# Gathering 17 instead of 13 target tiles in a graph network's first attention, most of them while the edge table is made

## The chip, the cores and the metric

The kernel runs on one core of a Trainium2 chip. The metric is the device time of one execution in microseconds. A core has TensorE (PE) for matrix products, VectorE (DVE), ScalarE (ACT) and GpSimd (POOL) for the rest, and SyncE (SP), which here only issues DMAs. Each engine takes its own instructions in the order in which they stand; semaphores tie the engines together. On-chip memory is SBUF, with 128 partitions, and PSUM, into which PE writes.

## The reference

There are 3125 nodes with 256 features and 50000 edges, sorted by target. Four graph layers alternate with four feed-forward blocks. Only the first graph layer and the routing behind it matter here:

```python
src, dst = with_self_loops(edge_index)
h = (x @ W.T).reshape(N, 4, 64)                # x is layer-normalized
e = leaky_relu(a_s[src] + a_d[dst], 0.2)       # a_s, a_d: one score a node and head
p = exp(e - segment_max(e, dst)[dst])
alpha = p / segment_sum(p, dst)[dst]
out = segment_sum(alpha[:, :, None] * h[src], dst)
x = x + elu(out + bias) + x_normalized
# then: layer norm, a router over 8 experts, the top 2 with their weights, their outputs added
```

## The kernel before

The 3125 nodes are 25 tiles of 128 rows, held in SBUF as `x`. The first graph layer, `gnn0`, has these stages.

*Projection.* Each tile is normalized, turned, and multiplied by the weights; `prepare` turns the scores into exponentials and writes the rows, with their scores, to DRAM as `scored` (ACT's queue).

*Edge table.* `table` makes a matrix with one column per target and one row per source that counts edges, in DRAM, for the first 19 of the 25 target tiles (`CONV`), which later convolutions use too. It goes over 152 windows of 16 targets. VectorE compares key numbers and writes one-hot tiles in 16 bits: `hi` for two windows at a time (L560, 128 x 2400), `lo` for eight windows (L552, 128 x 3072). PE multiplies them (L566, three products a window, into `pa`), ACT copies the counts to `cols` (L571), and SP writes blocks of 24 windows to DRAM (`ct<-cols`). Ten further comparisons, `same` (L478), count degrees. The table's function opens its own pools and closes them at its end.

*First attention*, `attend4`. A target tile is treated in one of two ways.

- Dense: `sweep` takes four target tiles at a time (a chunk). For each of the 25 source tiles it makes four `v` on VectorE (L857, maximum of two exponentials times the column of the table `c`, 128 x 512) and multiplies them on PE with the source rows (L917) and the denominators' row (L924). The table's columns come from DRAM by SP (`c<-ct`, five loads a chunk).
- Gathered: `GatheredAttention` fetches the rows of the actual edges. A target tile has 20 gathers of 128 rows, indirect DMAs on GpSimd's queue (L1873, `edge<-scored,from`), four to a buffer, with six buffers (`AHEAD`). Its five steps `some` each wait for the four gathers of a buffer: VectorE makes `factor` (L1921) and, in three steps of five, the product `edge<-edge,factor` (L1929); in the other two ACT makes it (L1926, 16 instructions); PE sums up (L1936, four products a step). `begin` makes the 0/1 matrices `hot` and `columns` first, for which SP loads `columns<-turned`.

Tiles from number `FIRST` on are gathered, 12 of 25 are dense, in three chunks. When a gathered step is due is set by due times: `times` has a start number, the time per tile (`each`), a delay and the time of the whole (`whole`), in planned microseconds; `upto(share)` runs all steps that are due at that share. The share is that of the dense steps done:

```python
steps += n
apart.upto(steps / (apart.start * NT))
for _ in range(apart.pace):
    if rest and s > 0:
        rest.pop(0)()
```

When two tiles are done, `experts.front` gives the pieces that route them (norm, transposes, router, place, and the sends to the experts' slots, two indirect DMAs a tile on GpSimd's queue, L2265); they go into `rest` and are run one or two after each dense step. After the last one come `schedule` and the first expert block.

A scheduler of the language then puts the instructions of each engine in an order of its own, by dependencies; the numbers of edges per target are prepared in `edges_by_column` for `GROUPED` groups of 32 targets, from tile `APART` on.

The call in `gnn0` stands after the table:

```python
early.close()
self.table(keep)
...
psum = self.pool(inner, "g0aps", 3, space=PSUM)
self.attend4(
    inner, "g0a", psum, hv, target, True, self.real, 1, done, self.scored[0],
    (FIRST, 30.0, -24.0, 420.0, 2), experts.front,
)
```

Of the kernel before, what the change touches and what calls it, by code (L numbers as in the profile page):

```python
# [32 lines left out]
P = 128  # L33
# [16 lines left out]
APART = 12  # L50

FIRST, SECOND, THIRD, CONV = 12, 12, 17, 19
# [31 lines left out]
class Net:  # L84
# [376 lines left out]
    def count_degrees(self, ctx, c):  # L461
# [28 lines left out]
        def sums():  # L490
# [7 lines left out]
            pm = one.tile([P, 512], F32, name="pm")  # L498
# [31 lines left out]
    def table(self, keep):  # L530

        nc = self.nc
        with ExitStack() as ctx:
            others = self.count_degrees(ctx, keep)
            acc = self.pool(ctx, "tabacc", 4, space=PSUM)
            lows = self.pool(ctx, "tablow", 2)
            hot = self.pool(ctx, "tabhot", 3)
            out = self.pool(ctx, "tabout", 2)  # L540
            keys = NT * WIN
            few, two = 8, 2
            block, end = 3 * P // WIN, CONV * P // WIN
            for w0 in range(0, end, block):
                n = min(block, end - w0)
                cols = out.tile([P, NT, block * WIN], BF16, name="cols")
                for w in range(w0, w0 + n):
                    if w % few == 0:
                        four = [P, few // two, P, two * TILES]
                        lo = lows.tile(four, BF16, name="lo")  # L550
                        of = self.lowt[:, w : w + few, :]
                        nc.vector.tensor_tensor(  # L552
                            lo, of.rearrange("p (q two) j -> p q (two j)", two=two).unsqueeze(2)
                            .to_broadcast(four),
                            self.keys6.unsqueeze(1).to_broadcast(four), op=ALU.is_equal,
                        )
                    if w % two == 0:
                        four = [P, two, keys, TILES]
                        hi = hot.tile(four, BF16, name="hi")
                        nc.vector.tensor_tensor(  # L560
                            hi, self.keyt[:, w : w + two, :].unsqueeze(2).to_broadcast(four),
                            self.keys3.unsqueeze(1).to_broadcast(four), op=ALU.is_equal,
                        )
                    pa = acc.tile([P, 512], F32, name="pa")
                    for j in range(TILES):
                        nc.tensor.matmul(  # L566
                            pa[:, :keys], lo[:, w % few // two, :, w % two * TILES + j],
                            hi[:, w % two, :, j],
                            start=(j == 0), stop=(j == TILES - 1),
                        )  # L570
                    nc.scalar.copy(  # L571
                        cols[:, :, (w - w0) * WIN : (w - w0 + 1) * WIN],
                        pa[:, :keys].rearrange("p (t d) -> p t d", d=WIN),
                    )
                    if others and w % 12 == 11:
                        others.pop(0)()
                nc.sync.dma_start(
                    self.ctm[:, :, w0 * WIN : (w0 + n) * WIN], cols[:, :, : n * WIN]
                )

# [247 lines left out]
    def sweep(self, ctx, name, nh, psum, hv, target, begin, step, finish, apart):  # L828
# [11 lines left out]
        def target_rows(t0, n):  # L840
            return self.target_rows(qpool, psum, target, t0, n, wide)
# [3 lines left out]
        q, rest = target_rows(*chunks[0]), []  # L845
        apart.rest = rest
        for i, (t0, n) in enumerate(chunks):
# [3 lines left out]
            for s in range(NT):  # L851
# [12 lines left out]
                apart.upto(steps / (apart.start * NT))  # L864
# [25 lines left out]
    def attend4(self, ctx, name, psum, hv, target, loops, need, flag, done, rows, times,  # L890
                ready=None):
# [6 lines left out]
        accp = self.pool(ctx, name + "acc", 1, space=PSUM)  # L898
# [57 lines left out]
        apart = GatheredAttention(self, ctx, name, psum, rows, target, times, finish_apart)  # L956

# [73 lines left out]
    def gnn0(self, experts):  # L1031
        nc, x = self.nc, self.x
        with ExitStack() as ctx:
# [5 lines left out]
            with ExitStack() as inner:  # L1039
                early = inner.enter_context(ExitStack())  # L1040
                keep = self.pool(inner, "tab", 1)
# [6 lines left out]
                edges = self.edges_by_window(inner, work, keep)  # L1048
# [23 lines left out]
                self.table(keep)  # L1072
            experts.begin(ctx)
            for load in experts.open_weights(0):
                load()

            def done(t, num, inv):
                rows = wk.tile([P, NH, HC], F32, name="rows")
                for h in range(NH):
                    nc.scalar.mul(rows[:, h, :], num[:, h, :], inv[:, h : h + 1])  # L1080
                r = rows.rearrange("p h c -> p (h c)")
                nc.vector.tensor_add(r, r, bias)
                grown = wk.tile([P, D], F32, name="grown")
                nc.scalar.activation(grown, r, AF.Exp)
                nc.scalar.activation(r, r, AF.Relu)
                nc.vector.tensor_add(x[:, t, :], x[:, t, :], r)
                nc.vector.scalar_tensor_tensor(
                    x[:, t, :], grown, 1.0, x[:, t, :], op0=ALU.min, op1=ALU.add
                )
# [1583 lines left out]
```

## Time and profile before

| | us |
|---|---|
| median of 3 runs | 4599.88 (4595.12 to 4603.21) |
| time of the profiled execution | 4597.16 |
| its span | 4595.4 |
| `hi` compares, first and last start | 106.0, 267.9 |
| first free gather, last gather (start) | 270.8, 694.6 |
| `v`, first and last start | 286.0, 738.6 |

Over the whole span PE is busy for 3727.8 us, DVE for 2503.1, POOL for 1625.9, ACT for 1221.7. Busy time of POOL counts its indirect DMAs[...], not the data's movement, and not the gap before the next issue. The median time of a gather is 1.010 us in the first attention, the shortest 0.942, the longest 6.762. The DMA column is the mean share in which the core's 16 DMA engines are busy.

### The profile page before, as it was taken

To read this page: it belongs to the slowest core of one execution; us is meant where nothing else is said; L and a number is where in the kernel's file an instruction comes from. 1 tells how busy PE (TensorE), PEld (TensorE's weight loads), DVE (VectorE), ACT (ScalarE), POOL (GpSimd) and SP (SyncE) were. 2 spreads that over 40 slices of the span, in tenths; PEclk is the share of its full clock that TensorE was granted. 3 is DMA by queue.
4 is the path that set the end of the run, shared out by engine and by line. 5 is a ranking of instruction groups with operands and counts; after the bars stand their busy time and mean duration, and the time that the engine had idled before them with its cause. 6 is when DMAs were issued, how large, how long until landed. Compare 5 with 4: busy or idle time off the path is not lost. (4 is left out here: it accounts for less than half of the span.)

```text
span 4595.4 us, 73195 instructions
## 1 busy us (share of the span) xinstructions
PE 3727.8 (81%) x25845; PEld 2022.9 (44%) x25942; DVE 2503.1 (54%) x8078; ACT 1221.7 (27%) x3841; POOL 1625.9 (35%) x1566
## 2 busy tenths in 40 slices
PE   5867775968887899999998999976599996865994
PEld 3322222543222667445444555544355554543552
DVE  7977886457765566767667421144432224533333
ACT  2433442323433111434333211100033332100331
POOL 2057772215774670000000365455311111463111
PEclk8889887989998999999998999998799998986997
DMA  4244433233443650000000465564511115443113
GB/s 125 86 143 120 122 104 92 79 109 108 126 123 94 168 144 19 2 2 2 2 2 27 140 169 165 150 216 121 147 32 29 29 29 164 130 137 81 54 52 108
DMA packets 356530, 431.28 MB, mean 94 GB/s; under 512 B 73207, under 2 KB 294063, under 8 KB 356161
## 3 DMA queue, kind: packets, MB, share of 16 engines
q0 software_dynamic: 73600, 199.97, 15.6%
q1 hardware_dynamic: 259344, 203.33, 15.2%
q10 hardware_dynamic: 23216, 23.17, 1.6%
q8 instruction: 217, 3.56, 0.3%
q14 instruction: 153, 1.25, 0.1%
HBM read 337.35 MB, written 90.59 MB: 93 GB/s over the span
## 5 line engine op out<-in xcount | busy, mean ns | idle before, releaser
L1873 POOL DMA_INDIRECT edge<-scored,from x680 | 770.3, 1133 | 482.5 <-PE pa L566 190.7
L1980 POOL DMA_INDIRECT edge<-rows,from x480 | 460.6, 960 | 338.7 <-issue 116.8
L2483 POOL DMA_INDIRECT results<-y,to x168 | 163.4, 973 | 892.9 <-DVE y L2482 580.7
L2477 PE MATMUL py<-w,ht 128*128 x1568 | 428.5, 388 | 21.1 <-DVE y L2482 17.6
L1668 PE MATMUL pz<-lstm_v,hist 128*32 128x192 f32 x7120 | 382.8, 333 | 30.5 <-DVE hist L1766 10.4
L2450 PE MATMUL ph<-w,xt 128*128 x896 | 385.9, 563 | 23.2 <-issue 12.6
L2469 ACT ACTIVATE ht<-pt,par 128x128 f32<-128x128 f32 x784 | 267.2, 366 | 442.1 <-PE pt L2466 441.7
L1926 ACT ACTIVATE edge<-edge,factor 128x65 f32<-128x65 f32 (+1 forms) x896 | 234.1, 348 | 432.6 <-DVE factor L1921 415.5
L1385 PE MATMUL acc<-c,hs 128*128 128x512 bf16 (+1 forms) x1458 | 328.7, 370 | 2.7 <-issue 1.3
L1430 PE MATMUL acc<-hs,c 128*128 128x512 bf16 x896 | 318.6, 398 | 5.2 <-DMA c<-ct 4.0
L2477 PEld LDWEIGHTS py<-w,ht 128*128 128x128 f32 x1568 | 259.2, 190 | 72.2 <-DVE y L2482 32.5
L1701 PE MATMUL pz<-pre,ident 128*128 128x192 f32 x900 | 268.6, 382 | 11.8 <-PEq L1774 11.8
L1793 POOL MEMSET hall<- 128x128 f32 x1 | 0.2, 204 | 772.3 <-DMA L_ffn_br<-in_L_ffn_br 772.3
L1434 PE MATMUL acc<-hs,c 128*128 128x256 bf16 x950 | 268.6, 283 | 4.6 <-issue 1.7
L2455 DVE COPY h<-ph 128x512 f32<-128x512 f32 (+1 forms) x224 | 139.7, 624 | 233.2 <-PE ph L2450 227.8
L1668 PEld LDWEIGHTS pz<-lstm_v,hist 128*32 128x32 f32 x7120 | 186.1, 109 | 181.3 <-DVE hist L1766 149.6
L2265 POOL DMA_INDIRECT slots<-rows,sloti x150 | 159.3, 1062 | 213.2 <-DVE sloti L2221 133.6
L2450 PEld LDWEIGHTS ph<-w,xt 128*128 128x128 f32 x896 | 158.1, 192 | 173.3 <-issue 113.0
L917 PE MATMUL acc<-v,g0hv 128*64 128x512 f32 x600 | 184.7, 712 | 58.6 <-DVE v L857 57.8
L1936 PE MATMUL edgeacc<-edge,hot 128*32 128x264 f32 (+1 forms) x1360 | 132.1, 427 | 112.5 <-DVE edge L1929 89.3
L857 DVE SCALAR_TENSOR_TENSOR v<-q,g0hv,c 128x512 f32<-128x512 f32 x300 | 216.7, 741 | 1.7 <-DMA c<-ct 1.6
L1385 PEld LDWEIGHTS <-hs 128*128 128x128 bf16 x1500 | 146.6, 99 | 158.6 <-issue 7.9
(489 smaller groups left out, 6349.2 us busy)
## 6 DMA issues: line engine op xcount, KB each, us to landing
c<-ct SPq DMA_DIRECT2D x116, 640.0 KB
slots<-slots SPq DMA_DIRECT2D x168, 129.0 KB
got<-results SPq DMA_DIRECT2D x24, 768.0 KB
w<-in_L_ffn_W SPq DMA_DIRECT2D x16, 1024.0 KB
ct<-cols SPq DMA_DIRECT2D x6, 2400.0 KB
c<-ct SPq DMA_DIRECT2D x25, 480.0 KB
edge<-scored,from POOLq DMA_INDIRECT x680
rows<-new ACTq DMA_DIRECT2D x20, 512.0 KB
```

Of the source, the lines that this page charges most:

```text
L857: nc.vector.scalar_tensor_tensor(to, q[:, h, :w], hv[:, s, h, D // nh + 1 : D // nh + 2], cols[s], op0=ALU.max, op1=ALU.mult,)
L1385: made = self.nc.tensor.matmul(acc[f][:, : n * P], lhs, cols[s], start=(s == 0 and i == 0), stop=(s == NT - 1), skip_group_check=True,)
L1430: nc.tensor.matmul(acc[t], lhs, hs[:, s, 0:2, :].rearrange("p i d -> p (i d)"), start=start, stop=stop, skip_group_check=True,)
L1434: return nc.tensor.matmul(acc[t][:, D:], lhs, hs[:, s, 2, :], start=False, stop=stop, skip_group_check=True,)
L1668: made = nc.tensor.matmul(pz[q * R : (q + 1) * R, :], s, m, start=start, stop=stop, tile_position=(0, q * R),)
L1701: made = nc.tensor.matmul(pz, self.ident, pre[:, g, s, :], start=True, stop=False)
L1873: nc.gpsimd.indirect_dma_start(out=tile[:, g, :], out_offset=None, in_=self.rows, in_offset=bass.IndirectOffsetOnAxis(ap=index, axis=0),)
L1926: nc.scalar.mul(part, part, factor[:, g, h : h + 1])
L1980: self.net.nc.gpsimd.indirect_dma_start(out=tile, out_offset=None, in_=self.rows, in_offset=bass.IndirectOffsetOnAxis(ap=index, axis=0),)
L2450: nc.tensor.matmul(ph[:, :wide], st["xt"][:, k, :], st["w1"][:, k * hid + c0 : k * hid + c0 + wide], start=(k == 0), stop=(k == KD - 1),)
L2469: nc.scalar.activation(ht[:, m, :], pt[:, cut], AF.Gelu, bias=st["par"][:, m : m + 1])
L2477: nc.tensor.matmul(py[:, :D], st["ht"][:, m, :], st["w2"][:, m * D : (m + 1) * D], start=(m == 0), stop=(m == nhc - 1),)
```

## The change

`APART` and `FIRST` go from 12 to 8: eight tiles are dense, in two chunks, and 17 are gathered. `table` no longer runs as a whole: it returns a list of 152 functions, one a window. They run in `attend4`, after the gathered attention has issued its first gathers, and after each of them the gathered steps that are due by then are run, and one waiting piece of the routing. The windows count for 0.57 of the planned time, the dense steps for the rest. The planned times change from (30, -24, 420) to (30, 6, 530). The table's pools move to the other side of SBUF, its blocks have 16 windows instead of 24, `pa` two PSUM buffers instead of four, `hi` two instead of three, and `pm` comes from the attention's pool. The experts' first weights get their memory earlier; their loads are called after the table.

```diff
-APART = 12
-FIRST, SECOND, THIRD, CONV = 12, 12, 17, 19
+APART = 8
+FIRST, SECOND, THIRD, CONV = 8, 12, 17, 19
...
-            pm = one.tile([P, 512], F32, name="pm")
+            pm = psum.tile([P, 512], F32, name="tp")
...
-            acc = self.pool(ctx, "tabacc", 4, space=PSUM)
+        acc = self.pool(ctx, "tabacc", 2, space=PSUM)
-            hot = self.pool(ctx, "tabhot", 3)
+        hot = self.pool(ctx, "tabhot", 2)
...
-            block, end = 3 * P // WIN, CONV * P // WIN
-            for w0 in range(0, end, block):
+        block, end = 2 * P // WIN, CONV * P // WIN
+        now = {}
+        def window(w):
+            if w % block == 0:
+                now["cols"] = out.tile([P, NT, block * WIN], BF16, name="cols")
...
+            if others and w % 12 == 11:
+                others.pop(0)()
+            if i == block - 1 or w == end - 1:
                 nc.sync.dma_start(
-                    self.ctm[:, :, w0 * WIN : (w0 + n) * WIN], cols[:, :, : n * WIN]
-                )
+                    self.ctm[:, :, (w - i) * WIN : (w + 1) * WIN], cols[:, :, : (i + 1) * WIN]
+                )
+        return [lambda w=w: window(w) for w in range(end)]
...
-        q, rest = target_rows(*chunks[0]), []
-        apart.rest = rest
+        q, rest = target_rows(*chunks[0]), apart.rest
...
-                apart.upto(steps / (apart.start * NT))
+                apart.upto(apart.share + (1 - apart.share) * steps / (apart.start * NT))
...
         apart = GatheredAttention(self, ctx, name, psum, rows, target, times, finish_apart)
+        if ahead:
+            ahead(apart)
+        accp = self.pool(ctx, name + "acc", 1, space=PSUM)
...
+            def ahead(apart):
+                with ExitStack() as ctx, self.tc.using_default_side("right"):
+                    windows = self.table(ctx, keep, psum)
+                    for i, window in enumerate(windows):
+                        window()
+                        apart.share = 0.57 * (i + 1) / len(windows)
+                        apart.upto(apart.share)
+                        if apart.rest:
+                            apart.rest.pop(0)()
+                edges.close()
+                for load in loads:
+                    load()
...
-                    (FIRST, 30.0, -24.0, 420.0, 2), experts.front,
+                (FIRST, 30.0, 6.0, 530.0, 2), experts.front, ahead,
```

## The prediction, made before the changed kernel had run

> **What bounds the kernel now.** The change touches the span up to the first expert block, about 806 us of 4595, so I read that stretch alone: first the busy time of each engine in its stages, then what VectorE and GpSimd wait for, then single instructions. The stages: the edge table is made (106 to 270 us), a turn-around (270 to 286), the dense steps of the first attention with the gathered targets among them (286 to 742), a tail (742 to 806).
>
> ```profile
> core 0: us, PE busy (x) PEld busy (x) DVE busy (x) ACT busy (x) POOL busy (x), PEclk, DMA share, GB/s
> 106.00:270.00 164.00, 137.41 (x533) 56.01 (x533) 163.54 (x110) 73.32 (x149) 6.23 (x1) 0.88 0.29 91
> 270.00:286.00 16.00, 4.73 (x29) 2.07 (x27) 6.26 (x17) 5.40 (x15) 9.02 (x9) 0.65 0.88 251
> 286.00:742.00 456.00, 343.45 (x1993) 93.91 (x1993) 357.55 (x991) 174.75 (x664) 342.97 (x294) 0.87 0.40 112
> 742.00:806.00 64.00, 18.97 (x70) 13.72 (x71) 30.34 (x145) 14.28 (x45) 11.42 (x14) 0.58 0.37 117
> ```
>
> The table is VectorE's alone (163.5 of 164 us), and GpSimd stands still in it. In the dense stage no engine looks full. But gaps between GpSimd's DMA issues are not counted as busy:
>
> ```profile
> 279.00:695.00 416.00, 329.65 (x284) 0.87 0.44 122
> ```
>
> ```profile
> DVE factor L1921 <- DMA edge<-scored,from: 78.7, 32, 5.8
> ```
>
> ```profile
> POOL edge L1873 <- issue: 63.7, 209, 0.3
> ```
>
> The first line is POOL alone in that stretch (busy, issues, clock, DMA), the others are waits from 286 to 742 (total, times, longest): 284 issues in 416 us, 329.65 us busy, and a gap of 0.30 us before each (63.7/209) makes 86 us more: 416. GpSimd is full from 279 to 695 us, at 1.465 us an issue, and VectorE loses 78.7 us waiting for gathered rows. So before, VectorE bounds the table, GpSimd the dense stage. Overlapping the two is what the change tries.
>
> What an issue costs beside a busy VectorE decides. The timeline of GpSimd and that of VectorE (start, us, engine, line):
>
> ```profile
> 263.77 6.76 POOL L1873 DMA_INDIRECT edge<-scored,from  x1 [190.67 <-PE pa L566]
> 270.84 0.95 POOL L1873 DMA_INDIRECT edge<-scored,from  x1 [0.30 <-issue]
> 283.21 1.97 POOL L1873 DMA_INDIRECT edge<-scored,from  x1 [0.30 <-issue]
> ```
>
> ```profile
> 262.72 6.98 DVE L560 TENSOR_TENSOR hi<-keyt,keys3s 128x2400 bf16<-128x2400 f16 x4
> 269.74 0.31 DVE L2159 COPY rows<-rowsto 128x2 f32<-128x2 f32 x3
> 283.12 1.24 DVE L1929 TENSOR_TENSOR edge<-edge,factor 128x1040 f32<-128x1040 f32 x1
> ```
>
> An undisturbed gather takes 0.95 us. The one at 283.21 began 0.09 us into a product of two SBUF tiles and took 1.97: it stood until the product's end (284.36) and then ran about 0.82. The one at 263.77, the only gather beside the table's compares, took 6.76: it stood through four `hi` compares and ended 0.8 us after the last. So a gather begun inside a two-input VectorE instruction waits for its end, and a run of 16-bit compares back to back was passed by in one piece. Over the dense stage the hold is 329.65/284 - 0.95 = 0.21 us an issue.
>
> **The change, part by part.** The sum is made against the profiled execution (span 4595.4, its time 4597.2, 2.7 below the median of the three runs, 4599.9).
>
> *Removed.* One of three dense chunks: 100 `v` at 0.683 us of spacing (four take 2.74), 68 us of VectorE, a third of L917 and L924 (94 us of PE), 5 loads `c<-ct`, 4 `q` copies.
>
> *Added.* Four gathered targets: 80 gathers on GpSimd, 20 `some` steps; a target costs VectorE some 6.5 us (three products at 1.17, five `factor` at 0.13, `hot` 0.75, `columns` 0.32, sum 0.34, the rest small), 26 us. Scaling on ACT is 32 x 0.336 = 10.7 us a target, PE 20 x 0.44 = 9, both on engines under half busy there. Four `columns` loads on SP of 160 KB. The per-target end (bias, exponent, normalization, routing, two sends) is done for every target either way.
>
> *Moved.* In the order in which the changed program's instructions stand, 48 of the 85 `some` steps, 204 GpSimd issues (192 gathers, 12 sends), and most of the matching front pieces come before the last `hi`. VectorE's list from first to last `hi` adds up to 279 us at the durations before (165 before); between last `hi` and first `v` 12; in the dense steps 221 (372 before). Total 512 against 544: 32 us less.
>
> *Start.* The scored rows are issued to DRAM until 100.2 us before. After, three `hi` and two `lo` stand ahead of the last of them, and the five `same` that stood there go later: I take 108 us for the first free gather; by then VectorE has done some 17 of its 279 us. Left: 262 us for 48 steps, 5.45 a step.
>
> *Table stage.* Each step needs 204/48 = 4.25 issues at 0.95 + 0.30 = 1.25 us when nothing holds them. Of the 5.45 us, 3.4 are 16-bit compares (76 `hi` at 1.745, 19 `lo` at 1.66, 10 `same` at 1.15, less those before the start), and in the order they stand in 91 runs, 1.9 a step. If a run is passed by whole, GpSimd gets in at each run's end, and about 0.35 times more in the other work: 2.25 issues. The other two run while VectorE waits for its rows: 2 x 1.25 = 2.5 us. A step takes 5.45 + 2.5 = 7.95 us, the stage 48 x 7.95 = 382, to 490 us. This is the wait that the change adds: `factor` on gathered rows, now with the next compares behind it on VectorE, the table's products on PE and its copies on ACT behind those. The whole table goes at the gathers' pace, 2.5 us a window instead of 1.08.
>
> Here a rule of the Trainium skill speaks otherwise. "SBUF — State Buffer", section "Who interferes with whom", has `tensor_tensor` without a two-port mode, contending with GpSimd's reads alone, and infers that descriptor generation needs the write interface. By that inference gathers run free beside `hi`: 204 x 1.25 = 255, so VectorE sets the stage at about 285 us (92% used). The rows say that an indirect DMA is held; it has an index to read, which would fit the page's first half. I take the rows.
>
> *Turn-around and dense stage.* From last `hi` to first `v` 16 us before (the wait for the last table write, 2.4 MB blocks and a 0.8 MB one; now ten blocks, the last again 0.8 MB): taken as equal. The remaining 168 issues (148 gathers, 20 sends) at 1.44 (a little under 1.465, since fewer products stand beside them) are 242 us, and after the last gather stand the last step and 12 `v`, 18 us: 260 from the end of the table. VectorE has 12 + 221 = 233 of work in it, so GpSimd still sets it. End at 490 + 260 = 750, against 742: +8.
>
> *Tail.* 64 us before; one more front pair stands in it (VectorE's list 26.3 against 20.9 us, with its chain through PE): +6.
>
> *Costed at nothing.* Two PSUM buffers for `pa` instead of four and two for `hi` instead of three: PE needs 0.9 us and ACT 0.49 a window, VectorE makes one in 1.08 now and 2.5 then; without that cover 0.2 us a window, 30 us. SP: `columns` loads stand among the table's writes, so a write waits behind a `columns` buffer that frees only with a gathered target; `cols` has two buffers of 16 windows (40 us at the new pace), and a block lost there costs up to one step, 8 us, once. The grouped numbers on 68 rows instead of 52 take the same instructions; `turned` is 2.8 MB instead of 2.1, 5 us more at the 122 GB/s of that stretch, needed some 30 us later. Expert weights, later attentions and convolutions keep their sizes.
>
> Sum: +8 + 6 = +14: 4611 for the profile, 4614 for the median.
>
> **The rivals.**
> 1. *The hold lets go at every compare's end* (place: each `hi`-`hi` boundary in the table stage). Then about 2.75 issues fit into the 5.45 us and 1.5 x 1.25 = 1.9 follow: 7.35 a step, 353 us, to 461; dense end 721, -21 + 6 = -15: 4585. For it: in the dense stage nearly all held gathers start at the next boundary, `v` to `v` too. Against: three boundaries passed at 263.77. It decides from 2.5 issues per step within VectorE's work: there the step is 7.7 us, the stage 368, and the sum with the tail zero.
> 2. *No hold, the page's inference*: 285 to 393, dense 260, end 653, -89 + 6: 4517. Against: both held rows.
> 3. *Compares and the small instructions between them hold as one run*: one issue a step gets in, 3.25 x 1.25 = 4.1 follow, 9.5 a step, 458 us; end 826, +90: 4690. For it: `factor` and the products have two SBUF inputs too, and stand back to back with `hi`. Against: gathers get in between products and `v` in the dense stage.
> 4. *It does not overlap*: the steps stand in the program before the last `hi`, but if rows land late enough that every step stops ACT, PE and the compares behind it, it joins case 3.
>
> **How the numbers follow.** Chances: forecast 0.34 (its own range 4595 to 4640), rival 1 0.28 (4560 to 4605), rival 2 0.13 (4500 to 4550), rival 3 with 4 0.25 (4650 to 4720). A measurement can tell about 0.2%, 9 us. Faster by more: all of rival 2, two thirds of rival 1, a little of the forecast's low end: 0.35. Within: 0.11. Slower: 0.54. The range, 4520 to 4695, leaves out half of rival 2 and the upper part of rival 3. It is wide because one row alone shows a gather beside compares.
>
> **What would show it.** Mean of the gathers before the last `hi`: near 1.6 us for the forecast (382/204 less the gap of 0.30), 1.4 rival 1, 1.1 or less rival 2, 1.9 rival 3. Last `hi` near 490; VectorE's wait for gathered rows some 120 us in the table stage; last `v` near 745; tail 70. The prediction is wrong if the last `hi` ends before 440 (the hold was overrated) or after 540, if in the dense stage GpSimd has gaps, or if the difference lies behind the first expert block.

## The result, and the profile after

The changed kernel takes 4616.52 us (median of 13 runs, 4607.79 to 4629.92) against 4601.45 for the kernel before, measured beside it (13 runs, 4595.12 to 4608.77): a ratio of 1.0035, with a 95% interval from 1.0025 to 1.0045. It is slower by 0.35%, about 16 us. The profiled execution took 4629.92 us, the longest of its 13, so I compare the two traces by the times at which things happen and not by their spans. At the first product of the first expert block (`ph`) the changed kernel is 14.4 us behind (807.6 against 793.2 us); what its profile loses after that (18.4 us more by the end of the span) is not in the medians.

The busy time of each engine by stage, of the kernel after (per window: length, then busy us and instructions of PE, weight loads, DVE, ACT, POOL, then the granted clock, the DMA share and the rate). The stages are: up to the first gather; the table with the gathered steps between its windows; the turn-around to the first `v`; the dense steps; the tail.

```profile
88.00:130.00 42.00, 4.09 (x86) 2.61 (x87) 20.97 (x26) 0.76 (x3) 0.30 (x1) 0.50 0.44 131
130.00:477.00 347.00, 219.44 (x1480) 88.01 (x1480) 253.10 (x433) 171.28 (x560) 283.63 (x209) 0.66 0.46 132
477.00:509.00 32.00, 9.04 (x46) 4.66 (x44) 13.03 (x43) 11.95 (x41) 24.08 (x27) 0.50 0.73 218
509.00:742.00 233.00, 200.10 (x1224) 55.71 (x1224) 212.27 (x549) 92.44 (x350) 177.95 (x146) 0.94 0.42 110
742.00:808.00 66.00, 14.54 (x59) 11.93 (x60) 35.24 (x175) 10.93 (x38) 14.03 (x15) 0.51 0.20 67
```

Read the POOL column of the second line: 209 issues, 283.63 us busy, 1.357 us each. With the gap of 0.30 us before each one (next fence) this is 209 x 1.66 = 347 us, the whole stage: GpSimd is full, while VectorE works for 253 of 347 us. In the dense stage and the turn-around 163 issues run from 476 to 723 us, 1.514 us each; VectorE works for 212 of the 233 us of the dense stage, so both are close to full there. The last dense product ends at 740.9, where it ended at 741.7 before. So 4 targets more and most of the gathers moved, and the dense stage ends at the same time. The loss arises after it: the tail is 66.7 us to the first `ph`, against 51.5.

The waits from 120 to 477 us (engine, line, what it waited for: total us, times, longest):

```profile
DVE factor L1946 <- DMA edge<-scored,from: 64.8, 21, 7.7
...
POOL edge L1898 <- DMA scored<-g0hv: 55.8, 1, 55.8
ACT cols L572 <- DMA turned<-short: 54.0, 1, 54.0
POOL edge L1898 <- issue: 51.5, 169, 0.3
...
DVE hi L560 <- PE pa L566: 40.9, 4, 39.5
```

The first row is the wait that the change adds, VectorE's for gathered rows: 64.8 us. The second, third and fifth are one thing that the forecast did not have: the first gather waits for the scored rows until 129.70 us, ACT's first copy of the table waits for the write of the grouped numbers (`turned<-short`), and through PE and its two buffers `pa` VectorE's `hi` waits too, 39.5 us at a stretch. GpSimd's timeline (start, us, engine, line, idle before it and what ended that):

```profile
129.70 0.98 POOL L1898 DMA_INDIRECT edge<-scored,from  x1 [55.81 <-DMA scored<-g0hv]
130.98 0.96 POOL L1898 DMA_INDIRECT edge<-scored,from  x1 [0.30 <-issue]
...
166.37 1.40 POOL L1898 DMA_INDIRECT edge<-scored,from  x1 [0.30 <-DMA edge<-scored,from]
```

And VectorE's timeline at the last of these:

```profile
165.16 3.54 DVE L560 TENSOR_TENSOR hi<-keyt,keys3s 128x2400 bf16<-128x2400 f16 x2
168.63 0.18 DVE L1946 TENSOR_TENSOR factor<-factor,edge 128x16 f32<-128x16 f32 x1
```

Two `hi` stand back to back from 165.16 to 168.70; the first ends at 166.99. The gather begun at 166.37 ended at 167.77, 0.79 us after the first `hi` and well inside the second. It got in at the boundary between two compares. So it goes for most gathers of this stage. Of the 101 gathers that have a `hi` or `lo` beside them 0.25 us after their start, 84 ended 0.79 to 0.83 us after the end of that one compare, 15 ended before it did and were not held, and two ended 2.53 us after it. Most of those compares have no other compare directly behind, so they say little about runs. Of the seven held gathers that have one, five got in at the boundary, and the two of 2.53 us stood through the next compare as well. The row on which the forecast rested, a gather that stood through four compares, is the other case. It is no accident of one trace: the first gather stands through four `hi` in all three profiles in which the table runs as a whole (6.76 us before, 6.79 in e2_rows68 and in e8_more). Why that one does not get in is not known.

### The profile page after: what moved, and what is told of

Same layout as the page of the kernel before. It is cut to its first block, busy times and chain, and to the rows that moved or that the text cites. A ratio compares the mean times of both kernels' runs of the same rounds, so it can differ in the third digit from the quotient of the medians.

```text
span 4628.2 us, 72963 instructions
## 1 busy us (share of the span) xinstructions
PE 3683.4 (80%) x25694; PEld 2015.9 (44%) x25694; DVE 2460.0 (53%) x8031; ACT 1243.0 (27%) x3962; POOL 1761.2 (38%) x1646
## 5 line engine op out<-in xcount | busy, mean ns | idle before, releaser
L1898 POOL DMA_INDIRECT edge<-scored,from x760 | 907.0, 1193 | 370.0 <-issue 203.3
L1951 ACT ACTIVATE edge<-edge,factor 128x65 f32<-128x65 f32 (+1 forms) x1024 | 267.5, 348 | 389.7 <-DVE factor L1946 356.0
L1453 PE MATMUL acc<-hs,c 128*128 128x512 bf16 x950 | 338.0, 400 | 4.8 <-DMA c<-ct 3.6
L1961 PE MATMUL edgeacc<-edge,hot 128*32 128x264 f32 (+1 forms) x1520 | 157.9, 456 | 134.8 <-DVE edge L1954 97.1
L566 PE MATMUL pa<-hi,lo 128*128 128x400 bf16 x456 | 156.5, 492 | 101.3 <-DVE hi L560 48.2
L1012 PE MATMUL acc<-g1bhv,v 128*128 128x257 f32 x850 | 204.5, 395 | 14.6 <-DVE v L860 8.4
```

The source lines that it names most:

```text
L1012: nc.tensor.matmul(a[:, : D + 1], v[0][:, j * P : (j + 1) * P], hv[:, s, 0, : D + 1], start=(s == 0), stop=(s == NT - 1),)
L1453: nc.tensor.matmul(acc[t], lhs, hs[:, s, 0:2, :].rearrange("p i d -> p (i d)"), start=start, stop=stop, skip_group_check=True,)
L1898: nc.gpsimd.indirect_dma_start(out=tile[:, g, :], out_offset=None, in_=self.rows, in_offset=bass.IndirectOffsetOnAxis(ap=index, axis=0),)
L1951: nc.scalar.mul(part, part, factor[:, g, h : h + 1])
```

## The experiments

The experiments fall into three groups of four, each with the kernel before measured beside it: 4596.75 us for e1 to e4, 4963.91 for e5 to e8, 4605.38 for e9 to e12. The second group ran on another chip, 8% slower for every kernel measured there; only its ratios are set beside the others.

| run | edit | us | ratio to before, 95% interval |
|---|---|---|---|
| after | the change | 4616.52 | 1.0035 [1.0025, 1.0045] |
| e1_split | `turned` written in two DMAs | 4608.98 | 1.0030 [1.0018, 1.0042] |
| e2_rows68 | before, 68 grouped rows | 4594.30 | 0.9996 [0.9988, 1.0004] |
| e3_short | `short` in memory of its own | 4615.85 | 1.0045 [1.0032, 1.0059] |
| e4_ten | 15 gathered targets | 4590.70 | 0.9990 [0.9981, 0.9998] |
| e5_ten48 | e4, fewer steps in the table | 4947.06 | 0.9966 [0.9951, 0.9982] |
| e6_twelve | 13 gathered targets, overlap alone | 4937.67 | 0.9940 [0.9917, 0.9963] |
| e7_halves | after, compares split in two | 4978.11 | 1.0024 [1.0008, 1.0040] |
| e8_more | before, 17 gathered targets | 5051.42 | 1.0175 [1.0153, 1.0198] |
| e9_halves | as e7_halves | 4602.22 | 1.0000 [0.9985, 1.0015] |
| e10_ten_halves | e4 and split compares | 4576.24 | 0.9937 [0.9917, 0.9957] |
| e11_twelve_halves | e12 and split compares | 4577.39 | 0.9943 [0.9921, 0.9965] |
| e12_twelve | as e6_twelve | 4592.74 | 0.9981 [0.9968, 0.9994] |

### The late start: e1_split, e2_rows68, e3_short

After, the first gather starts at 129.7 us where 108 was forecast. The suspect is the write of the grouped numbers, one DMA over 68 rows.

e1_split writes them in two pieces:

```diff
-        nc.sync.dma_start(
-            self.turned.rearrange("(w r) e -> w r e", r=GROUP),
-            short.unsqueeze(1).to_broadcast([GROUPED, GROUP, MANY * P]),
-        )
+        views = self.turned.rearrange("(w r) e -> w r e", r=GROUP)
+        for w0, w1 in ((0, 64), (64, GROUPED)):
+            nc.sync.dma_start(
+                views[w0:w1],
+                short[w0:w1].unsqueeze(1).to_broadcast([w1 - w0, GROUP, MANY * P]),
+            )
```

> The changed kernel with one edit: the write of `turned` (68 rows) is issued as two DMAs of 64 and 4 rows. Theory A (the 68-row write runs on few DMA engines, and scored rows, `columns` loads and the memory of `short` wait for it): the write lands near 105 us instead of 145, the first gather starts near 108 instead of 130, ACT's first `cols` copy no longer waits 54 us, last `hi` near 455 instead of 475, and the time is 20 to 30 us under the changed kernel, near 4590. Theory B (the scored rows are late because compares stand ahead of them): the first gather stays near 130, the time stays near 4616.

e2_rows68 gives the kernel before the 68 rows and nothing else of the change:

```diff
-APART = 12
+APART = 8
```

> The kernel before with APART = 8 alone: 68 grouped rows are prepared and written, FIRST stays 12, so nothing else moves. Theory A: the write takes some 60 us here too (landing near 145 instead of under 110); if `cols` lies in the memory of `short`, the table starts up to 36 us late (4637), otherwise nothing waits for it before 270 us and the time stays at 4601. Theory B: no difference in the write, 4601.

e3_short takes from ACT the reason to wait, by giving `short` memory that `cols` does not use again:

```diff
-        short = c.tile(sides, BF16, name="short")
+        short = keep.tile(sides, BF16, name="short")
```

> The changed kernel with `short` in the pool that lives on, so that `cols` cannot lie in its memory; the slow write stays. Theory A: ACT's 54 us wait and VectorE's 40 us stall in `hi` vanish, but the first gather stays at 130 and GpSimd sets the pace after it; VectorE has some 40 us more of compares done before the first gather, which takes hold time off the gathers (up to 18 us). Time between 4595 and 4612. If VectorE's stall itself set the time, 40 us less, near 4576.

Busy time by windows of e2_rows68, with the DMA share as the last column but one:

```profile
85.00:100.00 15.00, 6.83 (x245) 6.47 (x247) 14.39 (x19) 0.77 (x3) 0.00 (x0) 0.50 0.42 125
...
115.00:130.00 15.00, 13.37 (x48) 5.26 (x47) 15.00 (x10) 7.63 (x16) 0.00 (x0) 1.00 0.25 72
```

The same of the kernel before, with 52 rows:

```profile
85.00:100.00 15.00, 7.27 (x300) 7.08 (x300) 14.46 (x18) 0.77 (x3) 0.00 (x0) 0.50 0.77 203
...
115.00:130.00 15.00, 12.47 (x43) 4.89 (x42) 15.00 (x9) 6.89 (x14) 0.00 (x0) 0.89 0.00 0
```

And of e1_split:

```profile
85.00:100.00 15.00, 3.58 (x13) 1.78 (x13) 14.61 (x18) 0.77 (x3) 0.00 (x0) 0.50 0.84 170
```

In e2_rows68 the share from 115 to 130 us is 0.25: 4 of 16 engines, with the rest of this write and what was left of the scored rows. Before, the share was 0.77 from 85 to 100 and 0.00 from 115 on. In e1_split it is 0.84 at once, and ACT no longer waits for `turned`. The updates of the write's semaphore in the traces count the engines: behind the one at its issue come 4 in e2_rows68, the last at 141.2 us, and 13 before, the last at 100.5. The Trainium skill ("DMA: Bandwidth & Descriptors", section "Why a DMA increments its semaphore by 16 and not by 1") has a rule that fits: a DMA is spread over the largest number up to 16 that divides the size of the slowest dimension on both of its sides. For 68 rows that is 4, for 64 it is 16, for 52 it is 13; the share of 0.25 and the counts of 4 and 13 agree.

e2_rows68 also shows what this does to the scored rows. With nothing changed but the rows, the last update for them comes at 128.5 us, where it came at 111.1 before. It is 128.9 in after, and 110.5 in e12_twelve, with the overlap but 52 rows. So it is the write of 68 rows, and not the compares that now stand ahead, that makes the scored rows late. The total is no slower in e2_rows68 (0.9996), since there no gather starts before 264 us: the slow write costs only what the overlap makes wait for it.

What the start is worth e1_split does not show cleanly. It was expected near 4590, with the first gather near 108 us, and both failed. Its first gather goes at 122.7 us, released by another wait: the scheduler put VectorE's ten `same` ahead of `parts` there. Without that it could have gone little sooner, as the last of the scored rows is written at 121.9; why they are no sooner there, with the write quick, is open.

```profile
122.72 1.27 POOL L1900 DMA_INDIRECT edge<-scored,from  x1 [49.18 <-DVE parts L1862]
```

Of the 7 us gained the longer holds behind it took back 5 (206 issues of 1.684 us in the table stage instead of 209 of 1.658), the first `ph` came 1.9 us earlier than after, and the intervals of the two ratios overlap. The other kernels agree that the rows are the cause of most of the delay: the first gather starts at 129.7, 130.3, 125.9 and 126.0 us in the four profiles with the overlap and 68 rows in one write (after, e3_short, e7_halves, e9_halves), at 113.4 and 111.6 with 60 rows (15 engines; e4_ten, e10_ten_halves) and at 111.3 and 111.2 with 52 rows (e12_twelve, e11_twelve_halves).

In e3_short ACT's wait for `turned` is gone, and `hi` no longer waits for `pa`, but VectorE waits as long for the other user of the same write, the first `columns`:

```profile
DVE columns L1921 <- DMA columns<-turned: 40.4, 1, 40.4
```

The first gather, the pitch (the time from one issue to the next, 1.662 us) and the last dense product (741.2 us) stay, and the time of 4615.85 us lies above the expected 4595 to 4612. One reader of a late write was freed, and the next in the same queue took its place.

### The number of targets: e4_ten, e8_more, e6_twelve and e12_twelve, e5_ten48

e4_ten gathers 15 targets:

```diff
-APART = 8
+APART = 10
-FIRST, SECOND, THIRD, CONV = 8, 12, 17, 19
+FIRST, SECOND, THIRD, CONV = 10, 12, 17, 19
-                (FIRST, 30.0, 6.0, 530.0, 2), experts.front, ahead,
+                (FIRST, 30.0, 6.0, 470.0, 2), experts.front, ahead,
```

> The changed kernel with APART = FIRST = 10 and 470 planned microseconds: 15 gathered targets, 60 grouped rows, 10 dense targets in three chunks. Theory A: 60 rows spread over many DMA engines, so the write is quick and the first gather starts near 108; 40 gathers fewer on GpSimd (at 1.44 to 1.70 us each 60 us), VectorE 20 us more: end of the dense steps near 690, 4550. If the number of gathers did not bound, but VectorE or PE, the time would be at or over 4600.

e8_more makes the kernel before gather 17, without the overlap:

```diff
-APART = 12
+APART = 8
-FIRST, SECOND, THIRD, CONV = 12, 12, 17, 19
+FIRST, SECOND, THIRD, CONV = 8, 12, 17, 19
-                    (FIRST, 30.0, -24.0, 420.0, 2), experts.front,
+                    (FIRST, 30.0, -24.0, 500.0, 2), experts.front,
```

> The added targets alone: the kernel before with 17 gathered targets instead of 13, and no overlap with the table. Theory (GpSimd is the bound behind the table once 80 gathers are added): 340 gathers of 1.46 to 1.51 us from 264 on end near 770 instead of 695, against 36 us of VectorE's and TensorE's dense work less per 4 tiles; last acc product 765 to 790, total 4620 to 4650. Rival (dense and gathered work balance, as VectorE's saving of 4 dense tiles pays): last acc product about 742, total 4600 to 4610.

e6_twelve and e12_twelve are one kernel, the overlap alone with the 13 targets of before:

```diff
-APART = 8
+APART = 12
-FIRST, SECOND, THIRD, CONV = 8, 12, 17, 19
+FIRST, SECOND, THIRD, CONV = 12, 12, 17, 19
-                (FIRST, 30.0, 6.0, 530.0, 2), experts.front, ahead,
+                (FIRST, 30.0, 6.0, 410.0, 2), experts.front, ahead,
```

> The overlap alone: 13 targets gathered as before the change, over half of them between the steps of the table, nothing else moved. Theory (the gain of the overlap is real and the 4 added targets eat it): the table stage is about 260 x 0.6 = 156 gathers of 1.72 us long, 270 us, from about 109 to 385; behind it 27 dense tiles on VectorE, 330 us: last acc product about 720, total 4575 to 4580, faster than before by 0.4 to 0.6%. Rival (overlapping is worth nothing, since what the compares hold up of the gathers is what they hid): last acc product 740, total 4595 to 4600.

> The kernel of e6_twelve once more, as the pair of e11_twelve_halves: the overlap with 13 gathered targets and whole compares. Theory (the overlap gains, the 4 added targets eat it): ratio 0.993 to 0.996 as in e6_twelve, last acc product about 720 where the kernel before has 742. Rival (e6_twelve's gain belongs to the late results of TensorE on that chip, which weigh more on a kernel whose stages stand apart): ratio 0.998 to 1.001, last acc product about 740.

The added targets alone cost 1.75% (e8_more). Its busy time from first `v` to the last dense product, and GpSimd's gaps in the same window:

```profile
286.00:844.00 558.00, 339.64 (x1739) 94.13 (x1731) 306.77 (x892) 200.56 (x775) 402.53 (x368) 0.73 0.39 107
```

```profile
POOL edge L1873 <- issue: 90.8, 297, 0.5
```

VectorE has 307 us of work in 558, GpSimd 402.5 and 90.8 us of gaps: 371 issues from 271 to 831 us, 1.51 each. GpSimd is the bound, as expected, but the expectation came out too low (4620 to 4650 of 4600 us is 1.004 to 1.011): its end near 770 counts the 340 gathers alone, without the sends to the experts' slots that stand in the same queue. How much of the 1.75% belongs to the slower chip is not known. VectorE waits 156 us there in the first 1000 us of this profile with no releaser shown (more on this below), and the kernel before was not profiled on that chip.

The overlap alone gains 0.19% (e12_twelve; its interval reaches from 0.06 to 0.32%). e6_twelve had shown 0.6% on the slower chip, and that size did not come back, so I take e12_twelve; the expectation of 0.993 to 0.996 failed, and the rival's 0.998 came in, though the last dense product, at 734.6, lies between the two (720 and 740). Its windows show why the gain is small:

```profile
111.00:396.00 285.00, 196.17 (x1276) 79.33 (x1274) 228.37 (x352) 143.18 (x448) 236.30 (x160) 0.69 0.46 133
396.00:433.00 37.00, 7.48 (x55) 3.04 (x55) 10.17 (x26) 12.54 (x46) 28.49 (x28) 0.61 0.67 196
433.00:735.00 302.00, 275.69 (x1584) 75.28 (x1580) 280.53 (x708) 88.22 (x322) 138.28 (x113) 0.95 0.28 79
```

In the table stage GpSimd is full (160 issues of 1.78 us with the gap: 285), and VectorE is idle for 57 of 285 us. In the dense stage it is the other way: VectorE works for 280.5 of 302 us and GpSimd has done its gathers at 659. With the gathers of 13 targets over half done, the dense stage of three chunks is VectorE's. The overlap has moved idle time of VectorE, which was 98 us in the dense stage before, into the table stage and the turn-around, where it is idle for 27 of 37 us. And the mean gather in the table stage is 1.48 us against 1.16 of the dense stage before: each of 160 issues there costs 0.32 us more, 51 us of GpSimd in all.

With 15 targets (e4_ten) the table stage is 322 us, the dense one 277, with VectorE at work for 258.8 us of these: 0.10% faster than before. The expected 4550 us, with the dense steps done near 690, failed: they end at 741.0 as in after, since VectorE takes over as the bound. So the sign turns between 15 and 17 targets: 13 and 15 gain a little, 17 lose 0.35%. Not all of it is the targets' doing, as with 60 and 52 rows the first gather also starts 16 to 18 us earlier. At 17, in exchange for VectorE's work, GpSimd is full from the first gather to the last, 372 issues from 129.7 to 723.1, 1.595 us each.

The last part of the loss is in the tail. From last dense product to first `ph` it takes 64.7 to 67.1 us in the six profiles with 17 targets, 52.5 to 54.0 in the three with 15, 56.4 and 56.5 in the three with 13 and the overlap, 51.5 before. The timelines show where the 15.2 us of after arise. `g0adens` takes up the denominators of the last dense chunk; from it to `ph` there are 50.1 us before and 49.9 after. But before it stands 1.4 us behind the last dense product (741.68), and after 16.7 us (740.91). VectorE's timeline before:

```profile
743.08 0.17 DVE L932 TENSOR_TENSOR g0adens<-tp,g0aowns 128x16 f32<-128x16 f32 x1 [1.54 <-PE tp L967]
```

and after:

```profile
746.66 0.17 DVE L2184 COPY rows<-rowsto 128x2 f32<-128x2 f32 x1 [6.67 <-DMA slots<-rows,sloti]
...
757.61 0.17 DVE L935 TENSOR_TENSOR g0adens<-tp,g0aowns 128x16 f32<-128x16 f32 x1 [0.31 <-PE tp L973]
```

In the orders of VectorE and TensorE the routing of the last gathered tile, the odd one of 17, stands ahead of `g0adens`, and it begins with a wait of 6.67 us for rows to be sent to the slots. The distance from the last dense product to `g0adens` is 16.7 to 17.0 us in all five profiles with 17 targets and the overlap, 14.6 in e8_more, 7.4 to 9.0 with 15, and 6.6 with 13 and the overlap. How early the last gather ends does not decide it: in e7_halves it ends 36 us before the last dense product instead of 18, and the tail is 67.1 us. No run changed this order alone.

e5_ten48 puts fewer steps into the table stage of e4_ten:

```diff
-                        apart.share = 0.57 * (i + 1) / len(windows)
+                        apart.share = 0.48 * (i + 1) / len(windows)
```

> 15 targets gathered instead of 17 in the overlap (as in e4_ten), and a smaller part of them put into the table stage: the share of the gathered work that has to be done by the end of the table falls from 0.57 to 0.48. Theory (GpSimd's gathers, held by the compares, set the length of the table stage, and VectorE sets the length of the dense stage behind it): about 30 fewer gathers of 1.72 us lie in the table stage, last hi at about 385 instead of 435, then 460 to 475 gathers-and-dense work of the rest, GpSimd 145 + 30 gathers of 1.5 us and VectorE 275 us: last acc product near 700, total 4550. Rival (the total of VectorE's work over both stages sets the end, and moving steps from one stage to the other only moves idle time): what the table stage loses the dense stage gains, last acc product 730 to 741, total 4580 to 4592.

It ran on the slower chip, where e6_twelve's last dense product came 24.6 us later than in its twin e12_twelve. The table stage became 293 us long instead of 321, as both theories have it; the last dense product ended at 752.6, which less those 24.6 would be 728. Both this and the ratio, 0.9966, speak for the rival (4580 to 4592 of 4597 us is 0.996 to 0.999): what the table stage lost the later ones took back. But the twins e6_twelve and e12_twelve differ by 0.4% in their ratios, as much as is disputed here, so I leave it open.

### The length of a compare: e7_halves and e9_halves

If a gather waits for the end of the one compare in which it begins, shorter compares hold it for less. Every `hi` and `lo` is split into two instructions, with the same values written (for `lo` in the same way):

```diff
-                nc.vector.tensor_tensor(
-                    hi, self.keyt[:, w : w + two, :].unsqueeze(2).to_broadcast(four),
-                    self.keys3.unsqueeze(1).to_broadcast(four), op=ALU.is_equal,
-                )
+                one = [P, 1, keys, TILES]
+                for i in range(two):
+                    nc.vector.tensor_tensor(
+                        hi[:, i : i + 1],
+                        self.keyt[:, w + i : w + i + 1, :].unsqueeze(2).to_broadcast(one),
+                        self.keys3.unsqueeze(1).to_broadcast(one), op=ALU.is_equal,
+                    )
```

> The changed kernel with every compare of the table (hi and lo) split into two instructions of half the size. Theory (a gather issued beside a compare waits for the end of that one instruction, so the mean loss goes with the length of the instruction): the mean gather of the table stage falls from 1.36 to about 1.2 us, the pitch from 1.66 to about 1.5, the table stage from 347 to about 315 us, and with the last acc product at about 710 the total comes to 4585 to 4595. Rival 1 (a run of compares holds as one, the length of an instruction says nothing): mean stays at 1.36, total 4614 to 4620. Rival 2 (both engines take the memory in turns, and the loss goes with busy time): mean 1.36 to 1.38 as VectorE's busy time grows by the fixed cost of about 140 more instructions, total 4616 to 4625.

> The kernel of e7_halves once more, to have it where the kernel before takes about 4600 us as in the first four experiments. In e7_halves the mean gather of the table stage fell from 1.36 to 1.24 us, but VectorE and ScalarE waited 42 us and more there for results of TensorE that its records show as done, which no run of the first four had. Theory (the hold is per instruction, and without those late results the shorter gathers shorten the stage): mean 1.24 us, pitch 1.50 to 1.55, table stage 310 to 325 us instead of 347, total 4580 to 4592, ratio 0.996 to 0.998. Rival (the time the gathers no longer lose is lost to VectorE, which becomes the bound of the stage with 140 more instructions): pitch 1.62 to 1.66, total 4608 to 4620, ratio 1.002 to 1.004.

On the slower chip the mean gather of the table stage fell to 1.24 us, and the pitch stayed at 1.68. The waits of VectorE from 120 to 490 us show a kind that no profile of the other two groups has, "remote", where the profile finds no releaser; TensorE's records show the awaited results as done:

```profile
DVE factor L1936 <- remote: 42.0, 3, 20.8
```

What stops those engines there is not known; it is in all four profiles of that chip. Repeated where the kernel before takes 4605 us, as e9_halves, the pitch fell too. Its windows:

```profile
126.00:466.00 340.00, 225.56 (x1502) 89.42 (x1501) 261.68 (x529) 173.00 (x567) 274.44 (x216) 0.68 0.48 138
...
488.00:720.00 232.00, 203.20 (x1225) 56.77 (x1225) 212.22 (x550) 92.25 (x350) 178.38 (x147) 0.92 0.41 110
```

The mean issue is 274.44/216 = 1.27 us against 1.36, the pitch 1.57 against 1.66. The stage holds 7 issues more and ends 10.2 us earlier, all gathers end 21.3 us earlier (701.8 against 723.1), and `ph` starts 20.5 us earlier. The ratio is 1.0000, against 1.0035 of the change: the intervals do not meet, so the length of a compare is shown to set part of the time. The gain is smaller than expected (pitch 1.50 to 1.55, ratio 0.996 to 0.998). The groups of `hi` and of the gathers before the last `hi` (durations: shortest, median, longest in ns), first after:

```profile
L560 DVE TENSOR_TENSOR hi<-keyt,keys3s x73: 1790/1818/1899, 148.4 to 474.5; 128x2400 bf16<-128x2400 f16 x73
...
L1898 POOL DMA_INDIRECT edge<-scored,from x197: 942/1199/4229, 129.7 to 474.5; - x197
```

then e9_halves:

```profile
L564 DVE TENSOR_TENSOR hi<-keyt,keys3s x146: 950/980/1024, 145.3 to 465.1; 128x1200 bf16<-128x1200 f16 x146
...
L1903 POOL DMA_INDIRECT edge<-scored,from x204: 942/1008/4467, 126.0 to 464.3; - x102
```

The compares are little over half as long, and the median gather is nearly undisturbed. To see where the rest goes, I sorted the gathers by the VectorE instruction in which they begin, and summed what each took beyond 0.946 us:

| begun in | after: gathers, extra us | e9_halves: gathers, extra us |
|---|---|---|
| `hi` and `lo` | 101, 73.4 | 79, 42.0 |
| the product `edge` (1.23 us) | 11, 3.9 | 20, 15.7 |
| nothing (VectorE idle) | 56, 0.2 | 61, 0.1 |
| all | 197, 84.7 | 204, 63.8 |

The compares hold the gathers 31 us less, close to what their length promises, but 12 us come back: the gathers begin in the products instead, which have the same length as before. So both theories missed the size. VectorE did not become the bound (261.7 of 340 us).

### Both together: e10_ten_halves and e11_twelve_halves

The edits are those of e4_ten and of e12_twelve, with the split compares.

> 15 gathered targets (as e4_ten) and the split compares. Theory of the hold per instruction: table stage 187 issues x 1.55 = 290 us instead of 321, VectorE busy there 240 of 290; dense stage as in e4_ten (275 us, VectorE bound): last acc product at about 710, total 4560 to 4568, ratio 0.991 to 0.993. Rival (VectorE becomes the bound of the stage): 310 to 320 us, total 4585 to 4592, ratio 0.997 to 0.999.

> 13 gathered targets (as e6_twelve) and the split compares. Against e6_twelve, VectorE's work of the table stage (228 us of 284) lies close to what the stage would last with the shorter holds (159 issues x 1.55 = 246 us), so the gain is smaller than with 15 targets: 20 to 30 us by the theory of the hold per instruction, ratio 0.988 to 0.990 against 0.994 of e6_twelve. Rival (VectorE bounds the stage already): no gain, ratio 0.994.

e10_ten_halves takes 4576.24 us, ratio 0.9937 [0.9917, 0.9957]: faster than both kernels. Its windows beside those of e4_ten (first e4_ten, then e10_ten_halves):

```profile
113.00:435.00 322.00, 207.22 (x1301) 76.88 (x1297) 235.51 (x374) 154.80 (x499) 264.90 (x187) 0.63 0.44 129
...
464.00:741.00 277.00, 243.76 (x1611) 73.06 (x1611) 258.79 (x713) 94.17 (x351) 176.48 (x134) 0.94 0.32 90
```

```profile
112.00:408.00 296.00, 210.03 (x1355) 75.61 (x1352) 243.21 (x470) 154.90 (x500) 238.90 (x188) 0.67 0.48 140
...
434.00:708.00 274.00, 244.23 (x1611) 72.75 (x1611) 258.11 (x714) 93.18 (x350) 171.28 (x134) 0.95 0.34 91
```

Nearly the same number of issues in the table stage (187 and 188), 1.42 us each and then 1.27: the stage is 26 us shorter, the dense stage is VectorE's (258 of 274 us) and stays. The last dense product ends at 707.7 (expected: about 710), `ph` starts at 760.2, 33 us earlier than in the kernel before. The total was expected at 4560 to 4568 and came out 8 us above that (the ratio, 0.9937, just above 0.991 to 0.993); of the 33.8 us by which its `ph` starts earlier than e4_ten's, 23.2 are left at the end of the span, and what is lost on the way lies in parts that the edit does not touch. In e11_twelve_halves the table stage falls from 285 to 263 us, 233 of them VectorE's, and the ratio, 0.9943 [0.9921, 0.9965], is above the expected 0.988 to 0.990 because the expectation started from e6_twelve's 0.994; against e12_twelve's 0.9981 the gain is 0.4%, about 17 us.

## Why the prediction was right in its total, and wrong in its terms

The forecast was +14 us for 4614; 4616.52 came out. The median moved by 15 to 17 us, and the traces by 14.4 up to `ph`. But the terms missed, and the misses cancel (+21.7 at the start, -35.4 in the table stage, +4.6 behind it, +9.2 in the tail), which is luck:

| term | forecast, us | measured, us |
|---|---|---|
| first free gather | 108 | 129.7 |
| table stage from there | 382 | 346.6 |
| end of the table to the last dense product | 260 | 264.6 |
| last dense product | 750 | 740.9 |
| tail, more than before | +6 | +15.2 |

- *The bound of the table stage* was right: GpSimd's issue rate, not VectorE's list, sets it, as VectorE's work there is 253 us of 347. For the dense stage of 17 targets "GpSimd still sets it" is only half shown. GpSimd issues on to the end of its gathers (163 issues of 1.514 us, where 168 of 1.44 were taken), but VectorE waits for gathered rows only 6.2 us in the stage's 233 us, where it waited 78.7 before, and works for 212.
- *"a run of 16-bit compares back to back was passed by in one piece"* was wrong for the overlap, and with it the forecast's 2.25 issues within VectorE's work of a step: 145 of the stage's 209 issues stand beside a VectorE instruction 0.25 us after their start, 3.0 for each of 48 steps. Rival 1 was nearer in each of these terms: issues within VectorE's work (rival 1: 2.75), mean issue 1.357 us (rival 1: 1.4; forecast: 1.6), stage 346.6 us (rival 1: 353), wait for gathered rows 64.8 us (forecast: 120). Where compares do stand back to back, five of seven held gathers were let in at the boundary, and 21 of 22 with the compares split (e9_halves). The row at 263.77 was real, but it stands for the first gather beside a table that runs as a whole; to take it for every run of compares put 29 us into the sum (382 against rival 1's 353).
- *The start* was mis-sized at "costed at nothing": the 5 us for `turned` on 68 rows, worked out from bytes and a rate (122 GB/s, the mean of the 25 us from 75 to 100, of which the first 10 move nothing). The write ran on 4 engines instead of 13 and landed 60 us after its issue (85.9 to 145.6), where it was done at 100.5 before. The scored rows, written at the same time, came late with it and held the first gather back to 129.7 us, 22 us behind the forecast. The sum asked only when `turned` is needed ("needed some 30 us later"). It missed what else is written then: the overlap had moved the need for the scored rows from 264 us forward to the very time at which that write runs.
- *The rule of the Trainium skill* ("SBUF — State Buffer", "Who interferes with whom"), by whose inference gathers run free beside `tensor_tensor`, was rightly set aside: in the table stage of after, gathers with VectorE idle beside them take 0.949 us and those beside a `hi` 1.60, and shorter compares shorten them.
- *Turn-around*: 16 us were taken, 32.5 came. VectorE stands in its order, first for gathered rows, then for the routing's rows (timeline of after):

```profile
482.81 0.19 DVE L1946 TENSOR_TENSOR factor<-factor,edge 128x16 f32<-128x16 f32 x1 [6.32 <-DMA edge<-scored,from]
...
496.48 0.17 DVE L2184 COPY rows<-rowsto 128x2 f32<-128x2 f32 x1 [10.33 <-DMA slots<-rows,sloti]
```

  Behind these stand `inv`, ACT's `rows` (499.0), PE's transposes (502.3) and the first `v` (508.9). GpSimd went on through it, with 27 issues in 32 us, and the sum for the whole stretch, 260 against 264.6, was nearly right. Whether the turn-around cost anything at 17 targets is not shown, as VectorE is close to full behind it.
- *The tail* was too small by 9 us. That more routing would stand in it was right, but it was counted as some 5 us more of VectorE's work with its chain through PE. What came is the routing of one tile ahead of the dense targets' own, with a wait of 6.67 us for a send in it: 16.7 us from last dense product to `g0adens` where there were 1.4.
- *Nothing lost by fewer buffers*, as said: apart from its start VectorE waited 1.4 us for `pa` in the table stage, and ACT never for a block `cols` to be written.

Where did the expected gain of the overlap go? Into three things: the hold, 84.7 us of GpSimd in the table stage, which split compares cut by a quarter; the 80 gathers more, 1.75% by themselves on the slower chip, which the overlap has to pay first; and, with fewer targets, VectorE, whose work in the dense stage then sets the end. The 15 us that 17 targets lose stand in the tail.

## What to carry to other kernels

Before a step is moved ahead, look up what its inputs wait for at the new place: a transfer that was hidden for 150 us was on the path at once, and its time came from how many of the 16 engines its row count let it use, not from its bytes. When indirect DMAs on GpSimd are put beside VectorE's work, charge each one with the rest of the two-input instruction in which it begins, and make those instructions short before adding more gathers. A mechanism seen in one row of a trace deserves a rival of equal weight, and a total that comes out right says nothing about its terms. When a stage's end stays and the whole gets longer, look at the order of the first instructions behind it.

## What the runs showed of the hardware that I had not expected

- A write of 68 rows ran on a quarter of the DMA engines (share 0.25, 60 us), one of 52 rows, or of 64 and 4, on most of them (share 0.77 and 0.84 from 85 to 100 us).
- A hold mostly ends at the very end of one VectorE instruction, with the next one of the same kind right behind it: in e9_halves all 16 gathers that were held in a `hi` with another `hi` directly behind ended 0.79 to 0.80 us after the first one's end, and 21 of 22 when `lo` is counted in. The clearest exception is the first gather beside a table that runs as a whole (6.76 to 6.79 us, three profiles). An example, GpSimd's timeline and then VectorE's:

```profile
309.71 1.64 POOL L1903 DMA_INDIRECT edge<-scored,from  x1 [0.30 <-DVE same L478]
```

```profile
309.57 1.87 DVE L564 TENSOR_TENSOR hi<-keyt,keys3s 128x1200 bf16<-128x1200 f16 x2
```

- One chip was 8% slower for every kernel, with waits of up to 36 us in the first 1000 us, and up to 45 us later, for which the profile shows no releaser; a difference of 0.6% measured there was 0.2% elsewhere.
